# A four-layer graph network in one kernel: neighbours' lists made at fixed places of the convolution, and the attention's own rows scattered by order in the third layer's last step

## The chip, the cores and the metric

The kernel runs on one core of a Trainium2 chip. The metric is the device time of one execution in microseconds (us). The engines are TensorE (PE in the profile; PEld is its weight load), VectorE (DVE), ScalarE (ACT), GpSimd (POOL) and SyncE (SP). POOL and SP also issue DMAs: POOL the indirect ones, which gather or scatter rows of HBM by a list of row numbers, and SP the direct ones. A row L2049 of the profile is line 2049 of the kernel before.

## The reference, cut to what matters

Four layers follow one another on `x` of 8 batches x 2048 nodes x 64 features, float32, with one 0/1 adjacency `adj` (2048 x 2048). Each layer is `x = x + layer(relu(layernorm(x)))`. The change touches what surrounds layers 1 to 3:

```python
# layer 1: Chebyshev convolution, K = 3
A_stack = [I, A, 2 A A - I]
w = einsum('nd,dkio->nkio', embedding, weight); b = embedding @ bias
x_g = einsum('knm,bmc->bnkc', A_stack, x)
out = einsum('bnki,nkio->bno', x_g, w) + b
# layer 2: three steps of message passing
for _ in range(3):
    effects = einsum('nm,bmd->bnd', adj, v)
    v = relu(concat([v, effects]) @ W1.T + b1) @ W2.T + b2
# layer 3: graph attention
h = x @ weight; e_src = h @ a[:D]; e_dst = h @ a[D:]
e = adj * leaky_relu(e_src[:, :, None] + e_dst[:, None, :], 0.2)
out = softmax(e, -1) @ h + bias
```

The product of `adj` with a [2048, 64] matrix per batch is needed in layers 1 and 2 (two products in layer 1, three in layer 2), and the softmax of layer 3 runs over all 2048 nodes, those that are no neighbours having the score 0. The adjacency is sparse: only a few nodes have many neighbours.

## The kernel before

**Tiles and columns.** A node's 8 x 64 values stand in one row of 512 columns (CW). The 2048 nodes make 16 tiles of 128 (NT), and four chunks of four tiles for work that has the features on the partitions. The first tile holds the nodes with many neighbours.

**A product with the adjacency (class `Feed`).** Each of the three steps of layer 2, and each of the two products of layer 1, gathers 60 blocks of 128 rows (`raw<-sent,index`, 256 KB, L2636, on POOL), splits each into two parts (`part_hi` by ACT, L2653, `part_lo` by DVE, L2654), and multiplies both by weights of 0 and 1 on PE (`acc`, L177). There are six buffers for raws in the Chebyshev product and the steps, so a gather waits for the `part_lo` that reads the buffer's last content. Rows of nodes with many neighbours are kept in SBUF (`hub`) and are multiplied densely.

**Layer 1 (`layer1_near`, then `convolution_near`).** First the Chebyshev product over 16 tiles, then the convolution at four places, one for each chunk (order 1, 0, 2, 3). A place has four column blocks q, each with four groups (`blk`, two blocks b a group); a group makes four `pk` in PSUM by eight matmuls (six PSUM buffers, `Conv.bank`), then four `y` on DVE (L1856: (pk + bias) x emb, three buffers), each of which is added to an accumulator `half` (L1863): on POOL, but on DVE where b is the last. The second product of the adjacency runs alongside, one place ahead (`advance()`, twice a group). The layer norm of a finished chunk is done in pieces, in the following place (the list `waiting`). The first q of the first place is computed early (`Conv.first_part`, `early0_*`, `early_y`).

**Layer 2 (`layer2_near`).** Three steps over 16 tiles. The generator `neighbours` (L2015) goes along with steps 0 and 1, one piece (`near_step`) after each group of four gathered blocks. It first sorts the nodes by their number of neighbours (`ranks`, L493, a running sum by nine adds at L521; `by_rank`, L537) and stores the order in HBM (`order3`). Then, for each of tiles 1 to 15 in that order, it fetches 128 rows of 0/1 links (L2039, a POOL gather of 512 KB), multiplies them by the node's number plus one (L2043), and takes the eight greatest numbers of each row (MAX8, L2049), as often as the tile's longest list needs (one to three times), with a MATCH_REPLACE (L2052) between; a copy (L2056) puts the numbers into `near`. 15 multiplications, 21 MAX8 and 6 MATCH_REPLACE in all. In step 2, class `Scores` normalises each chunk as its rows come out, multiplies by the weight of layer 3 and writes rows of h and scores to HBM (`f_rows`, L2899 and L2900).

**Layer 3 (`layer3_near`, class `Near`).** The first tile, in the sorted order, is done densely: 16 blocks `jt`, each with 16 exponentials on ACT (L3119, L3120), a maximum and a multiplication on DVE (L3123, L3124), then a `plain` matmul and 16 recordings of `first` on PE. The other 15 tiles (`others`, in the order 15, 13, 11, 1, 10, 2, 9, 3, 8, 4, 7, 5, 6, 12, 14) go by lists: for each tile one gather of the tile's own rows (`ring<-f_rows,order`, by order) and 3 to 20 gathers of its neighbours' rows (`ring<-f_rows,near`, L2966, POOL), a softmax over the list (from `e`, L3011, to `den`), products `y` of two neighbours at a time (L3037), which PE adds up in `acc` with an identity, `o` (L3056), and a scatter of `o` to `att_rows` by order (L2977). The two generators take turns in the program. At the end `result` reads `att_rows` and adds x.

**What sets the order.** Each engine takes its instructions in order. A scheduler puts them in that order when the kernel is built, from the program's order and its own estimates of when inputs are ready; `behind` (L193) makes an instruction keep its place in the program's order on its engine. Pools of buffers (`bufs`) add waits for release.

The lines of the convolution (L1861 to L1863) and of layer 2 that hand out this work:

```python
own = b == NBLK - 1
add = nc.vector if own else nc.gpsimd
add.tensor_add(acc, acc, y)
...
for i, _ in enumerate(feed.listed(acc, t)):
    if i % feed.GROUP == feed.GROUP - 1 or i == (LISTED[t] or FAR) - 1:
        near_step()
```

Of the kernel before, what the change touches and what calls it, by code (L numbers as in the profile page):

```python
# [7 lines left out]
F = mybir.dt.float32  # L8
BF = mybir.dt.bfloat16

F12 = mybir.dt.float32r
I32 = mybir.dt.int32
# [7 lines left out]
P = 128  # L20
# [115 lines left out]
class Kernel:  # L136
# [8 lines left out]
    def __init__(self, tc, ctx, a):  # L145
# [19 lines left out]
        self.f_rows = dram.tile([N, WIDE], F, name="f_rows")  # L165
        self.att_rows = dram.tile([N, NB * D], F, name="att_rows")
# [1516 lines left out]
    def layer1_near(self, slots, k2, far):  # L1683
# [11 lines left out]
        with (  # L1695
# [4 lines left out]
            with tc.tile_pool(reuse_waits="tile", name="cheb", bufs=2) as w:  # L1700
# [13 lines left out]

                feed = Feed(self, lists, w, self.sent[0], lambda jt: ah(jt))
                for t in range(NT):
                    acc = ps.tile([P, CW], F, name="acc", bufs=2)
                    feed.target(acc, t, hub)
                    if t < HUBS:
                        nc.scalar.copy(ah(t), acc)  # L1720
                        lists.hub.fill(self, t, ah(t))
                    else:
                        feed.finish(ah(t), ah(t), acc, t)
                    nc.sync.dma_start(self.sent[1][t * P : (t + 1) * P], ah(t))
                    if t > 0:
                        turn(t - 1)
                    if t == NT // 2:
                        conv.begin()
# [5 lines left out]
    def convolution_near(self, slots, k, ps, conv):  # L1734
# [7 lines left out]
        with tc.tile_pool(reuse_waits="tile", name="conv", bufs=2) as w:  # L1742
# [62 lines left out]
            steps.prepare(bank)  # L1805
            for place, ch in enumerate(chunks):
                s = slice(ch * CW, (ch + 1) * CW)
                aah = aahs[place % 2]
                ends = place == NC - 1
                ahead = iter(()) if ends else product(place + 1)  # L1810
# [12 lines left out]
                for q in range(NP):  # L1823
# [6 lines left out]
                    for blk in range(0, NBLK, 2):  # L1830
# [17 lines left out]
                        for b in (blk, blk + 1):  # L1848
                            for half in range(2):
# [10 lines left out]
                                if new:  # L1860
                                    own = b == NBLK - 1  # L1861
                                    add = nc.vector if own else nc.gpsimd
                                    add.tensor_add(acc, acc, y)  # L1863
# [17 lines left out]
                waiting[2:2] = [first, lambda: None, lambda norm=norm: next(norm, None)]  # L1881
            while waiting:
                waiting.pop(0)()
# [19 lines left out]
    def layer2_near(self, slots, k2):  # L1903
# [3 lines left out]
        with (  # L1907
# [8 lines left out]
            near = self.neighbours(k, lambda: ps.tile([P, CW], F, name="p2"), slots)  # L1916
# [60 lines left out]
            def near_step():  # L1977
                next(near, None)

            for step in range(3):  # L1980
                if step == 2:
                    for _ in near:
                        pass
                feed = Feed(self, lists, w, self.sent[2 + step], None)
                for t in range(NT):
# [11 lines left out]
                    for i, _ in enumerate(feed.listed(acc, t)):  # L1997
                        if i % feed.GROUP == feed.GROUP - 1 or i == (LISTED[t] or FAR) - 1:
                            near_step()
                        advance(2 if step == 2 and t in (13, 14) else 1)  # L2000
# [14 lines left out]
    def neighbours(self, k, bank, slots):  # L2015

        nc = self.nc
        order = k.tile([P, 2, NT], I32, name="order")  # L2020
        w = Parts(slots.tile([P, 2 * N], F, name="sort", tag="q4"))
        rank = self.ranks(w, bank, 1, NEAR[1])
        yield
        self.by_rank(w, bank, rank, order)
        nc.sync.dma_start(self.order3, order)
        yield
        near = self.near
        words = slots.tile([P, 2, N], F, name="near_rows", tag="q4")
        rows = words[:, 0].bitcast(BF).rearrange("p (i n) -> p i n", i=2)
        named = words[:, 1].bitcast(F16).rearrange("p (i n) -> p i n", i=2)  # L2030
        words = slots.tile([P, 2, N], F, name="line", tag="q5")
        whole = words[:, 0].bitcast(I32)
        line = words[:, 1, : N // 2].bitcast(F16)
# [3 lines left out]
        for t in range(1, NT):  # L2037
            raw, row = rows[:, t % 2], named[:, t % 2]
            nc.gpsimd.indirect_dma_start(  # L2039
                raw, None, self.links[:],  # L2040
                bass.IndirectOffsetOnAxis(ap=order[:, 1, t : t + 1], axis=0),
            )
            nc.vector.tensor_mul(row, raw, line)  # L2043
# [3 lines left out]
            for i in range(most):  # L2047
                eight = top[:, 8 * i : 8 * i + 8]
                nc.vector.max(out=eight, in_=row)  # L2049
                yield  # L2050
                if i + 1 < most:
                    nc.vector.match_replace(  # L2052
                        out=row, in_to_replace=eight, in_values=row, imm_value=0.0
                    )
                    yield
            nc.vector.tensor_copy(near[:, FIRST[t] : FIRST[t + 1]], top[:, : NEAR[t]])  # L2056

# [644 lines left out]
class Conv:  # L2702
# [5 lines left out]
    def __init__(self, kern, slots, k, ps):  # L2708
# [19 lines left out]
        for j in range(2):  # L2728
# [9 lines left out]
        self.accs = [  # L2738
            [k.tile([P, CW], F, name=f"early{q}_{half}") for half in range(2)]
            for q in range(self.EARLY)  # L2740
        ]
# [21 lines left out]
    def first_part(self):  # L2763
# [3 lines left out]
        for q in range(self.EARLY):  # L2767
            for b in range(NBLK):
                for half, src in enumerate(self.xs):
# [3 lines left out]
                    y = self.k.tile([P, CW], F, name="early_y", bufs=2) if b else acc  # L2773
# [59 lines left out]
class Scores:  # L2833
# [30 lines left out]
    def chunk(self, col, first, n):  # L2864
# [18 lines left out]
        for t in range(first, first + n):  # L2883
# [17 lines left out]
            yield  # L2901

# [13 lines left out]
class Near:  # L2916
# [52 lines left out]

    def leave(self, t, o):  # L2970

        self.back.append((t, o))
# [9 lines left out]
    def block(self, t):  # L2982
# [9 lines left out]
        self.fetch(block[:, 0], self.order[:, 1, t : t + 1])  # L2992
# [5 lines left out]
    def others(self):  # L2998
# [3 lines left out]
        for place, t in enumerate(self.TILES):  # L3002
# [8 lines left out]
            nc.vector.tensor_tensor(  # L3011
                e, block[:, :, NB * D : NB * D + NB], es.unsqueeze(1).to_broadcast(full),
                op=OP.add,
# [47 lines left out]
    def first_tile(self):  # L3061
# [24 lines left out]
        self.fetch(mine, self.order[:, 1, :1])  # L3086
# [27 lines left out]
        for jt in range(NT):  # L3114
# [8 lines left out]
            nc.vector.tensor_max(m, m, m2)  # L3123
# [153 lines left out]
```

## Time and profile before

| | |
|---|---|
| three runs | 1938.78, 1944.40, 1930.53 us (median 1938.78) |
| the profiled execution, its own time | 1938.07 us |
| its span from the first to the last instruction | 1936.3 us |
| mean granted clock of TensorE | 0.933 of full speed |
| layer 0 | to about 600 us |
| Chebyshev product, its gathers | 604 to 700 us |
| convolution, places 1 to 3 | 886 to 1216 us |
| steps 0 and 1 of layer 2, their gathers | 1249.9 to 1351.6 and 1375.6 to 1475 us |
| layer 3 | 1655 to 1936 us |
| HBM traffic | 240.40 MB read, 63.14 MB written |

How to read it: busy time is the sum of an engine's instructions; a group's line gives its line in the kernel, engine, operation, what it writes <- what it reads, shapes, how often, its busy time and the mean of one in ns, then the engine's idle time just before it and whose result ended that idle time. In the table by stage each engine's column is its busy us and, in brackets, its instructions; the last three columns are the granted clock, the mean busy share of the 16 DMA engines and what they moved in GB/s.

### The profile page before, as it was taken

Reading aid. Unit: us, or ns where it says so; the run is one execution under the profiler, and the core shown is the slowest. Engines: PE = TensorE matmul, PEld = TensorE weight load, DVE = VectorE, ACT = ScalarE, POOL = GpSimd, SP = SyncE. Lnnn points to the kernel's source line nnn. Section 1 sums busy time; section 2 is a strip of 40 time slices with the busy share of each in tenths; the row PEclk is TensorE's granted clock in tenths of the full one; section 3 lists DMA queues with packets and bytes.
Section 4 is the critical chain, followed back from the end, with each engine's and each line's share of the span. In section 5 each row is a group of like instructions: output and inputs, shape, how many; then the busy total and the mean of one; then the engine's idle time right before and its main releaser. Section 6 shows DMA issues by size and latency. Waiting matters only on the chain. (4 is left out here: it accounts for less than half of the span.)

```text
span 1936.3 us, 22507 instructions
## 1 busy us (share of the span) xinstructions
PE 1695.0 (88%) x7139; PEld 972.7 (50%) x7139; DVE 1407.0 (73%) x2312; ACT 818.9 (42%) x1650; POOL 1048.6 (54%) x1007
## 2 busy tenths in 40 slices
PE   6888999998997788999999999689799899679885
PEld 2445766664334544443443444467577576345432
DVE  6888788874667688776776656788888576458874
ACT  5732544454656644222111100366666654356300
POOL 1101466677753646876656456276474641577770
PEclk8898999998987898999999989879989999789887
DMA  9741223335535864242230210478788774766665
GB/s 342 278 122 46 76 88 109 104 116 186 173 111 166 240 193 151 71 108 83 59 110 28 88 42 24 167 233 269 227 266 269 218 243 157 233 178 175 183 173 199
DMA packets 127226, 305.22 MB, mean 158 GB/s; under 512 B 29536, under 2 KB 33392, under 8 KB 121968
## 3 DMA queue, kind: packets, MB, share of 16 engines
q0 software_dynamic: 45328, 149.60, 26.2%
q1 hardware_dynamic: 79456, 149.81, 23.3%
q10 hardware_dynamic: 2304, 4.20, 0.6%
q8 instruction: 60, 0.98, 0.2%
q14 instruction: 78, 0.64, 0.1%
HBM read 240.40 MB, written 63.14 MB: 157 GB/s over the span
## 5 line engine op out<-in xcount | busy, mean ns | idle before, releaser
L2636 POOL DMA_INDIRECT raw<-sent,index x300 | 320.0, 1067 | 277.0 <-DVE part_lo L2654 114.9
L2653 ACT CAST part_hi<-raw 128x512 fp32r<-128x512 f32 x352 | 213.8, 619 | 325.6 <-PE acc L177 212.5
L2654 DVE TENSOR_TENSOR part_lo<-raw,part_hi 128x512 fp32r<-128x512 f32 x352 | 266.1, 780 | 92.3 <-ACT part_hi L2653 82.6
L177 PE MATMUL pk<-q,w 128*128 128x512 f32 (+1 forms) x768 | 303.3, 608 | 2.0 <-DVE q L1750 0.9
L1863 POOL TENSOR_TENSOR half<-half,y 128x512 f32<-128x512 f32 x180 | 230.3, 1308 | 120.2 <-DVE y L1856 119.6
L177 PE MATMUL acc<-q,ident 128*128 128x512 f32 x416 | 202.8, 613 | 23.1 <-DVE q L3056 17.0
L177 PE MATMUL acc<-part_lo,weights 128*128 128x512 f32 x365 | 167.0, 459 | 34.2 <-DVE part_lo L2654 33.7
L177 PE MATMUL acc<-part_hi,weights 128*128 128x512 f32 x365 | 173.6, 479 | 22.2 <-ACT part_hi L2653 21.7
L177 PEld LDWEIGHTS pk<-q,w 128*128 128x128 f32 (+1 forms) x768 | 115.5, 189 | 152.4 <-issue 117.4
L1856 DVE SCALAR_TENSOR_TENSOR y<-pk,bias,q 128x512 f32<-128x512 f32 x210 | 148.1, 744 | 54.9 <-PE pk L177 36.7
L2966 POOL DMA_INDIRECT ring<-f_rows,near x121 | 141.7, 1171 | 64.6 <-issue 29.2
L177 PEld LDWEIGHTS acc<-q,ident 128*128 128x128 f32 x416 | 77.0, 194 | 96.8 <-issue 42.9
L177 PEld LDWEIGHTS acc<-part_lo,weights 128*128 128x128 f32 x365 | 73.1, 200 | 87.9 <-DVE part_lo L2654 74.2
L2345 POOL TENSOR_TENSOR q<-q,beta 128x512 f32<-128x512 f32 x57 | 76.0, 1335 | 71.3 <-DVE beta L2321 32.6
L177 PEld LDWEIGHTS acc<-part_hi,weights 128*128 128x128 f32 x365 | 72.8, 199 | 71.4 <-ACT part_hi L2653 39.6
L177 PE MATMUL pp<-adj,x_ind_hi 128*128 128x512 f32 x256 | 89.5, 465 | 0.5 <-DVE q L882 0.3
L300 DVE RECIPROCAL std<-std 128x512 f32<-128x512 f32 (+1 forms) x17 | 53.8, 3162 | 32.6 <-ACT std L299 32.6
L3037 DVE TENSOR_TENSOR q<-ring,e 128x1024 f32<-128x1024 f32 x58 | 70.1, 1220 | 9.0 <-PE acc L177 8.8
L2622 ACT CAST hub_weights<-dense 128x384 fp32r<-128x384 uint8 x80 | 40.5, 511 | 84.1 <-PE acc L177 83.6
L2345 POOL TENSOR_TENSOR q<-q,coef 128x512 f32<-128x512 f32 x57 | 63.0, 1106 | 21.0 <-DVE q L2368 17.6
L2553 POOL DMA_INDIRECT listed_raw<-in_adjT_dram,cell x60 | 63.8, 1063 | 16.5 <-issue 16.1
L177 PE MATMUL pp<-adj,x_ind_lo 128*128 128x512 f32 x256 | 72.7, 403 | 0.0
(510 smaller groups left out, 3482.3 us busy)
## 6 DMA issues: line engine op xcount, KB each, us to landing
rows<-in_adj_dram SPq DMA_DIRECT2D x16, 1024.0 KB, 8.9
adj_t<-in_adjT_dram SPq DMA_DIRECT2D x64, 256.0 KB, 3.0
own<-sent SPq DMA_DIRECT2D x52, 256.0 KB, 4.1
raw<-sent SPq DMA_DIRECT2D x52, 256.0 KB, 3.5
sent<-u SPq DMA_DIRECT2D x48, 256.0 KB, 4.0
q<-x SPq DMA_DIRECT2D x9, 1024.0 KB, 5.0
links<-squares POOLq DMA_DIRECT2D x16, 512.0 KB, 8.0
sent<-q SPq DMA_DIRECT2D x32, 256.0 KB, 3.6
```

What stands on the lines that cost most here:

```text
L177: self.nc.tensor.matmul(out, lhsT, rhs, start=start, stop=stop)
L300: nc.vector.reciprocal(std, std)
L1856: nc.vector.scalar_tensor_tensor(y, pks[b, half], bias[:, b : b + 1], emb[:, b], op0=OP.add, op1=OP.mult,)
L1863: add.tensor_add(acc, acc, y)
L2345: self.nc.gpsimd.tensor_tensor(x, x, by.unsqueeze(2).to_broadcast([P, NB, D]), op=OP.mult)
L2553: self.kern.behind(nc.gpsimd.indirect_dma_start(raw[:, i], None, rows, bass.IndirectOffsetOnAxis(ap=self.cell[:, c + i : c + i + 1], axis= ...
L2622: self.nc.scalar.copy(to, self.lists.dense[:, :, i * P : (i + 1) * P])
L2636: self.nc.gpsimd.indirect_dma_start(raw, None, self.rows[:], bass.IndirectOffsetOnAxis(ap=self.lists.index[:, c : c + 1], axis=0),)
L2653: nc.scalar.copy(hi, raw)
L2654: nc.vector.tensor_sub(lo, raw, hi.bitcast(F))
L2966: self.nc.gpsimd.indirect_dma_start(to, None, self.kern.f_rows[:], bass.IndirectOffsetOnAxis(ap=index, axis=0))
L3037: nc.vector.tensor_tensor(y.rearrange("n i (b f) -> n i b f", b=NB), block[:, i : i + 2, : NB * D].rearrange("n i (b f) -> n i b f", b=NB) ...
```

## The change

1. The sort (`order_nodes`, from the first half of `neighbours`) runs in the Chebyshev product instead of at the start of layer 2, a piece after each of the tiles 2 to 4, in pools of its own. Layer 2 loads the order back, twice, by SP.
2. The lists are made in places 1 to 3 of the convolution, one piece after every group, with DVE's multiplications, MAX8 and MATCH_REPLACE kept in the program's order. A gather of links is issued one tile ahead. The rows of links share a buffer with the early part of the convolution, which is over by then.
3. The adds of the last b go to POOL, as all others.
4. In step 2, each tile's rows of h and scores are also scattered to two new tensors, `own_h` and `own_scores`, at the nodes' places in the order: 32 indirect DMAs on POOL.
5. In layer 3 the tiles' own rows are read from those by SP (two direct DMAs a tile) instead of 16 gathers on POOL; `e` and the first tile's maximum keep the program's order on DVE.

```diff
+        self.own_h = dram.tile([N, NB * D], F, name="own_h")
+        self.own_scores = dram.tile([N, 2 * NB], F, name="own_scores")
...
+                sorting = self.order_nodes(conv.bank, conv.order)
                 feed = Feed(self, lists, w, self.sent[0], lambda jt: ah(jt))
...
+                    if t > 1:
+                        next(sorting, None)
...
             for place, ch in enumerate(chunks):
...
+                if place == 1:
+                    words = k.tile([P, 4 * CW], F, name="near_rows", tag="early", bufs=1)
+                    near = self.neighbours(
+                        steps.k, conv.order, range(1, NT),
+                        words.bitcast(BF).rearrange("p (i n) -> p i n", i=2),
+                        words.bitcast(I32), w.tile([P, N], F16, name="line", bufs=1),
+                    )
...
-                                    own = b == NBLK - 1
-                                    add = nc.vector if own else nc.gpsimd
-                                    add.tensor_add(acc, acc, y)
+                                    nc.gpsimd.tensor_add(acc, acc, y)
+                        if b % 2:
+                            next(near, None)
...
-            near = self.neighbours(k, lambda: ps.tile([P, CW], F, name="p2"), slots)
+            order = k.tile([P, 2, NT], I32, name="order")
+            nc.sync.dma_start(order, self.order3)
+            self.nodes = k.tile([P, 2, NT], I32, name="order")
+            nc.sync.dma_start(self.nodes, self.order3)
...
-                    for i, _ in enumerate(feed.listed(acc, t)):
-                        if i % feed.GROUP == feed.GROUP - 1 or i == (LISTED[t] or FAR) - 1:
-                            near_step()
+                    for _ in feed.listed(acc, t):
                         advance(2 if step == 2 and t in (13, 14) else 1)
...
+    def order_nodes(self, bank, order):
+        rank = order[:, 1].bitcast(F)
+        with self.tc.tile_pool(reuse_waits="tile", name="sort", bufs=1) as w:
+            self.nc.vector.tensor_copy(rank, self.ranks(w, bank, 1, NEAR[1]))
         yield
-        self.by_rank(w, bank, rank, order)
-        nc.sync.dma_start(self.order3, order)
+        with self.tc.tile_pool(reuse_waits="tile", name="sorted", bufs=1) as w:
+            self.by_rank(w, bank, rank, order)
         yield
+        self.nc.sync.dma_start(self.order3, order)
+        yield
+    def neighbours(self, k, order, tiles, rows, whole, line):
...
+        fetch(0)
+        for i, t in enumerate(tiles):
+            fetch(i + 1)
+            row = rows[:, i % 2].bitcast(F16)
+            self.behind(nc.vector.tensor_mul(row, rows[:, i % 2], line))
             yield
...
+                self.behind(nc.vector.max(out=eight, in_=row))
                 yield
...
+        early = k.tile([P, 4, CW], F, name="early", tag="early", bufs=1)
+        self.accs, self.ys, self.turn = [[early[:, 0], early[:, 1]]], early[:, 2:], 0
+        self.order = k.tile([P, 2, NT], I32, name="order")
...
+            at = bass.IndirectOffsetOnAxis(ap=kern.nodes[:, 0, t : t + 1], axis=0)
+            nc.gpsimd.indirect_dma_start(kern.own_h[:], at, self.rows(t), None)
+            nc.gpsimd.indirect_dma_start(kern.own_scores[:], at, kern.scores[:, t], None)
...
+    def own(self, to, t):
+        dma, rows = self.nc.sync.dma_start, slice(t * P, (t + 1) * P)
+        dma(to[:, : NB * D], self.kern.own_h[rows])
+        dma(to[:, NB * D :], self.kern.own_scores[rows])
...
-        self.fetch(block[:, 0], self.order[:, 1, t : t + 1])
+        self.own(block[:, 0], t)
...
-            nc.vector.tensor_tensor(
-                e, block[:, :, NB * D : NB * D + NB], es.unsqueeze(1).to_broadcast(full),
-                op=OP.add,
+            kern.behind(
+                nc.vector.tensor_tensor(
+                    e, block[:, :, NB * D : NB * D + NB], es.unsqueeze(1).to_broadcast(full),
+                    op=OP.add,
+                )
             )
...
-        self.fetch(mine, self.order[:, 1, :1])
+        self.own(mine, 0)
...
-            nc.vector.tensor_max(m, m, m2)
+            kern.behind(nc.vector.tensor_max(m, m, m2))
```

## The prediction

> **What bounds the kernel now.** I read the page's table of engines first, then the busy time of each engine by stage, then the groups of instructions inside three stages, and last the waits of VectorE (DVE) in the fourth layer. The whole-span table says only that PE is busy 88% of the time; the stages have different limits, so the change has to be costed stage by stage.
>
> ```profile
> PE 1695.0 (88%) x7139; PEld 972.7 (50%) x7139; DVE 1407.0 (73%) x2312; ACT 818.9 (42%) x1650; POOL 1048.6 (54%) x1007
> ...
> core 0: us, PE busy (x) PEld busy (x) DVE busy (x) ACT busy (x) POOL busy (x), PEclk, DMA share, GB/s
> 604.00:700.00 96.00, 76.08 (x275) 48.74 (x273) 68.18 (x109) 64.09 (x134) 62.12 (x60) 0.90 0.82 233
> 886.00:1000.00 114.00, 113.07 (x363) 47.66 (x363) 79.60 (x102) 17.68 (x36) 73.42 (x62) 1.00 0.28 79
> 1000.00:1110.00 110.00, 108.98 (x344) 43.43 (x342) 72.86 (x95) 15.14 (x29) 60.73 (x49) 1.00 0.20 60
> 1110.00:1216.00 106.00, 103.79 (x347) 46.11 (x346) 66.37 (x94) 5.97 (x10) 57.77 (x48) 0.95 0.09 35
> 1250.00:1352.00 102.00, 87.34 (x464) 69.07 (x463) 89.91 (x122) 61.82 (x123) 72.76 (x66) 0.90 0.79 244
> 1376.00:1476.00 100.00, 86.41 (x459) 68.53 (x458) 85.33 (x115) 62.83 (x125) 73.23 (x68) 0.93 0.82 259
> ```
>
> Row 604 is the Chebyshev product, rows 886 to 1110 are places 1 to 3 of the convolution, rows 1250 and 1376 are steps 0 and 1 of the third layer. In the convolution PE is busy 326 of 330 us, and DVE only 219: DVE has 111 us to spare, POOL 138. In the two steps DVE is near 87% and POOL's DMA issues follow one another. So the change moves DVE work from two stages where DVE and POOL set the pace to one where PE does.
>
> ```profile
> L2636 POOL DMA_INDIRECT raw<-sent,index x60 | 65.1, 1085 | 33.7 <-DVE part_lo L2654 18.8 <-issue 11.0 <-DVE near L2056 1.5
> L2654 DVE TENSOR_TENSOR part_lo<-raw,part_hi 128x512 fp32r<-128x512 f32 x62 | 40.9, 690 | 12.4 <-ACT part_hi L2653 9.6 <-ACT hub_weights L2622 2.0 <-PE acc L177 0.2
> ...
> L2049 DVE MAX8 top<-q 128x8 f32<-128x2048 f16 x9 | 20.6, 2286 | 0.0
> ...
> L2043 DVE TENSOR_TENSOR q<-q,q 128x2048 f16<-128x2048 bf16 x9 | 11.0, 1217 | 0.0
> ```
>
> These are groups of step 1 (1376 to 1476). POOL's raw gathers wait 18.8 us for part_lo (the buffer it frees), and part_lo stands on DVE behind MAX8s of 2.29 us.
>
> ```profile
> L177 PE MATMUL pk<-q,w 128*128 128x512 f32 (+1 forms) x488 | 199.2, 609 | 2.0 <-DVE q L1750 0.9 <-DVE y L1856 0.7
> L1863 POOL TENSOR_TENSOR half<-half,y 128x512 f32<-128x512 f32 x136 | 173.4, 1303 | 112.5 <-DVE y L1856 112.2
> L1856 DVE SCALAR_TENSOR_TENSOR y<-pk,bias,q 128x512 f32<-128x512 f32 x158 | 111.6, 744 | 45.7 <-PE pk L177 32.2 <-POOL half L1863 11.9 <-PE side L177 0.5
> ...
> L2654 DVE TENSOR_TENSOR part_lo<-raw,part_hi 128x512 fp32r<-128x512 f32 x22 | 29.0, 1318 | 16.2 <-ACT part_hi L2653 16.2
> L1863 DVE TENSOR_TENSOR half<-half,y 128x512 f32<-128x512 f32 x24 | 26.5, 1109 | 3.0 <-POOL half L1863 1.1
> ```
>
> These are groups of the convolution's places 1 to 3. PE waited 2.0 us for anybody. The same part_lo that takes 690 ns in step 1 takes 1318 here, among POOL's adds.
>
> ```profile
> DVE e L3011 <- DMA att_rows<-o,order: 15.1, 1, 15.1
> DVE e L3011 <- DMA ring<-f_rows,near: 14.3, 3, 9.4
> ...
> DVE e L3011 <- DMA ring<-f_rows,order: 8.5, 1, 8.5
> ```
>
> These are DVE's waits in the fourth layer (waiting instruction, releaser: total us, times, longest). POOL issues 153 indirect DMAs there back to back from 1660 to 1884; the 15.1 is a tile's `e` standing at the head of DVE's queue while the first tile's work, ready, stands behind it.
>
> **The sort.** About 13.5 us of DVE (nine compares of 0.526, one of 2.29, small ones) leave the start of step 0, where they stand among 19 part_los between 1236 and 1264; the order's store on SP goes along. In the Chebyshev product DVE is busy 71%, but DMA is 0.82 and POOL issues steadily, waiting for part_lo. Hidden by DVE's 28 us of idle time it costs nothing; with the cover gone 13.5. I take +4 there. At step 0's start POOL waited up to 10.4 us on part_lo; I take -4 of it.
>
> **The convolution.** Into places 1 to 3 go on DVE 15 multiplications (1.217), 21 MAX8 (2.286), 6 MATCH_REPLACE (2.277), 15 copies (0.17), one cast (1.16): 18.3 + 48.0 + 13.7 + 2.6 + 1.2 = 83.8 us. Out go 24 adds of 1.109 (26.6). DVE: 219 + 57 = 276 of 330. Per group of four y, of which the three places have 48, that is 5.75 us where PE needs 330/48 = 6.9. POOL gets those 24 adds (1.3 each, 31 us) and 15 gathers (some 1.3 with their gap, 20 us) and an iota (1.8): 192 + 53 = 245 of 330. On the mean PE keeps its lead. It does not at the norms: the group with a MAX8 beside a reciprocal (3.3 us) and its neighbours comes to 11.4, another of the same norm to 10.7, against 7. PE has six pk banks, four of them one group's, so it can run about two banks (3.5 us) ahead of a late DVE: of the 4.4 + 3.7 us some 4 go through to PE. Three norms: 12.
>
> Here a rule speaks against the change. The row: part_lo, two inputs from SBUF, takes 1318 among POOL's adds against 690, so +0.6 us. The Trainium skill, "SBUF — State Buffer", section "Who interferes with whom", says why it may be worse: a DVE instruction with two SBUF inputs and a GpSimd instruction that reads SBUF exclude each other, and the later one is blocked for the whole of the other. The new multiplication has two SBUF inputs and 32 more adds run on POOL (30 in the places, two early ones); MAX8 and MATCH_REPLACE, with one large input, are free of it. By the row 15 x 0.6 = 9 us of DVE (285 of 330, 5.9 a group, still under 6.9); by the rule a multiplication can stand behind a run of adds, and the longest part_lo of this stage, 3.5 us, is 2.8 over its plain time, so 15 x 2.8 = 42 and DVE at 318 of 330, where PE would lose perhaps 40. I take the row, as it is this stage's mean: +12 in all, 0 to 40 for the range. A gain is excluded, since PE only idles 2 us.
>
> **Steps 0 and 1.** 14 gathers (1.07 + 0.3 gap, 19 us of POOL), the iota and about 75 us of DVE leave. The raws of step 0 take 1249.9 to 1351.6 and of step 1 1375.6 to 1475, some 102 and 100 us. POOL's own pace is 60 x (1.085 + 0.3) = 83. The nearest row is the Chebyshev product, the same 60 raws without lists: 94 us. The steps have more small matmuls (464 against 275 records), PE busy 87 at most. I take 92 each: 202 - 184 = -18. Bounds: 97 each (-8, only what POOL waited for the lists' own work), 83 each (-36). Late next is the raw's landing and the part_hi on ACT.
>
> **Step 2.** 32 scatters on POOL, about 1.35 each, 43 us. POOL is 45% busy or less from 1545 to 1600 and 5 of 40 after, PE is 95% busy, so they lie beside PE. But a scatter that waits for its rows holds the raws queued behind it, and 4 MB more are written where DMA stands at 0.78. Behind the last step's end only the pair of the last tile is left, 2.7 us. I take +3 (0 to 12). The order's two loads on SP are early and hidden.
>
> **Layer 3.** POOL loses 16 gathers (1.03 + 0.3, 22 us) of a queue that is full for 224 us. SP reads the rows instead, 32 direct DMAs, in time beside the ring's gathers. The program order on `e` and on the first tile's maximum puts three blocks of first-tile work before tile 15's `e`, which fills the 15.1 us stall; but tiles no longer overlap: each begins its softmax after the last one's `o`, a chain of 1.4 us before the first product and about as much at its end, 2.8 x 15 = 42 us in which PE has only the first tile's matmuls. Those (16 blocks of about 3.5 us with `plain`) fill most of it. Laid along DVE and PE the tiles end near 1887 instead of 1901: -14. Bounds -25 (stalls and gathers both go) and +10 (the gaps between tiles are not filled).
>
> Sum: 4 - 4 + 12 - 18 + 3 - 14 = -17 from the profiled execution's 1938.07, so 1921. That execution is 0.7 below the median of the three runs (1930.5 to 1944.4), so nothing is corrected.
>
> **Rivals.** (1) Slower: the convolution becomes bound by DVE. The place is y L1856 behind a MAX8; it decides when the groups' sum on DVE stays over 6.9 us for longer than two pk banks last. If all that was added shows, 57 + 9 = 66 in place of 12: 1975; half of that gives 1942. For it: the 11 us groups at the norms, two-input multiplications among adds. Against: 54 us of idle DVE left by the rows. (2) Little gain: the steps are held by DMA (0.8) and PE, 97 each, and layer 3's gaps eat what POOL saves (0): 1938 + 4 - 4 + 12 - 8 + 3 = 1945; with half of layer 3's gain 1938. For it: raws land late and POOL issues at its pace already; against: the Chebyshev row. (3) Large gain: steps at POOL's pace (-36), layer 3 -25, conv +5: 1938 + 5 - 36 + 3 - 25 = 1885. (4) It doesn't do what it says: if the lists fell out of the convolution into its tail, the 57 us of DVE would come after 1216. The instruction order of the changed kernel has all of them between the y's, so little is left for this.
>
> **How the numbers follow.** The summed case (1903 to 1938) has 0.48, the large gain 0.16, little gain 0.16, the slower case 0.20. A difference of 1% (19 us) is about what a measurement of this kernel can tell from no change. Faster by over 1% (under 1919): 0.16 and somewhat over half of the first, 0.28, so 0.44; slower (over 1958): of the fourth case the larger part and a little for what none of them names, 0.17; within: 0.39. The range leaves out a tenth on each side: 1890 to 1960.
>
> **What would show it.** Right: PE's idle time in the convolution's pk group grows from 2 to about 15 us, at the groups after a norm; raws of steps 0 and 1 span 90 to 95; L2043's mean in the convolution about 1.8; e L3011 waits no longer for att_rows. Wrong: PE waiting on y by 40 us or more (rival 1), raws still at 97 (rival 2), the last scatter of attention rows more than 245 us after the last step's end, as before.

## The result, and the profile after

| | before | after |
|---|---|---|
| median of the runs on one chip | 1935.08 us (4 runs) | 1969.74 us (4 runs, 1965.26 to 1972.78) |
| ratio after / before, 95% interval | | 1.0168 (1.0137 to 1.0200) |
| span of the profiled execution | 1936.3 us | 1971.0 us |
| mean granted clock | 0.933 | 0.930 |

The change makes the kernel slower by 1.7%, 33 us by the ratio. The forecast was 1921, with 1890 to 1960 as range. Set out by stages, with the start of each read from the timelines (POOL's raw gathers, SP's last write of rows of h to `f_rows`, the span's end), the two profiled executions differ so:

| stage | before | after | difference | forecast |
|---|---|---|---|---|
| first raw gather of the Chebyshev product to first raw gather of step 0 | 645.1 | 670.9 | +25.8 | +12 (sort +4 and -4, convolution +12) |
| steps 0 and 1, to the first raw gather of step 2 | 246.6 | 213.1 | -33.5 | -18 |
| step 2, to the last write of `f_rows` | 157.7 | 168.4 | +10.7 | +3 |
| layer 3, to the end | 282.1 | 314.2 | +32.1 | -14 |

(604.8 before and 604.4 after lie ahead of them.) The signs are right in three stages, and the lists' gain is even greater than forecast. Layer 3 has the wrong sign and is 46 us off.

The table by stage of the kernel after, rows in the columns shown before: two stretches of the convolution's places 1 to 3 (which run, by their first `y`, from 882, 1004 and 1122; before from 868, 982 and 1097), steps 0 and 1, step 2, the start of layer 3 and its tiles. The stretches don't hold the same work as the prediction's rows.

```profile
912.00:1033.00 121.00, 116.02 (x363) 47.98 (x362) 99.40 (x119) 18.19 (x36) 89.69 (x74) 0.99 0.29 89
1033.00:1158.00 125.00, 122.11 (x364) 49.80 (x364) 92.29 (x116) 12.63 (x24) 82.04 (x66) 0.95 0.27 78
...
1275.00:1383.00 108.00, 101.07 (x566) 81.40 (x565) 69.50 (x107) 75.68 (x151) 62.62 (x60) 0.98 0.81 255
1383.00:1488.00 105.00, 98.42 (x559) 80.97 (x559) 68.00 (x104) 75.06 (x149) 60.83 (x60) 0.97 0.81 253
...
1489.00:1657.00 168.00, 149.62 (x701) 98.04 (x701) 102.78 (x202) 87.06 (x182) 90.24 (x90) 0.96 0.68 215
1657.00:1711.00 54.00, 25.61 (x116) 16.87 (x116) 14.52 (x29) 23.33 (x68) 37.75 (x36) 0.74 0.79 254
1711.00:1937.00 226.00, 185.85 (x526) 90.68 (x526) 161.19 (x289) 74.57 (x243) 132.93 (x106) 0.89 0.50 141
```

In the first stretch of the convolution DVE now works 99.4 of 121 us (82%) and PE still 116: it is not bound by DVE. In the steps PE is at 94%, DVE at 65%. Step 2 has 90 instructions on POOL where there were 61. The row that decides is the last: from the first `e` to the last scatter 226 us pass in which nobody is busy throughout: PE 82%, DVE 71%, POOL 59%. The same stretch of the kernel before is as long, but POOL is at 74% in it:

```profile
1672.00:1901.00 229.00, 193.83 (x641) 102.65 (x641) 165.09 (x307) 96.25 (x309) 170.43 (x146) 0.91 0.61 172
```

The clocks of the two stretches, 0.89 and 0.91, make some 4 us of PE's time (an estimate: 186 x (0.91 / 0.89 - 1)).

Who waits in layer 3 of the kernel after (waiting instruction, releaser: total us, times, longest):

```profile
POOL att_rows L3000 <- DVE e L3035: 40.7, 5, 13.9
...
DVE o L3081 <- PE acc L179: 31.6, 14, 7.0
...
PE acc L179 <- DVE e L3050: 24.3, 9, 3.2
DVE q L3062 <- PE acc L179: 23.2, 19, 2.3
...
DVE q L3099 <- DMA q<-in_adj_dram,order: 18.8, 1, 18.8
...
PE acc L179 <- DVE q L3081: 12.2, 5, 3.6
```

L3035 is `e`, L3050 the last but one step of the softmax, L3081 `o` and the first two products, L3062 the products. The waits of `e` for DMAs (15.1, 14.3 and 8.5 us before) are gone, as the change meant. In their place DVE waits for PE at the end of 14 of the 15 tiles, 31.6 us (before: 3.8 in three), and PE waits for DVE at the start of the next, 24.3 + 12.2 (before, L3056 alone: 17.0). The scatters that wait for `e` are the same thing from POOL's side. DVE's timeline at one tile's end:

```profile
1726.58 2.35 DVE L3062 TENSOR_TENSOR q<-ring,e 128x1024 f32<-128x1024 f32 x2
1735.95 0.69 DVE L3081 TENSOR_TENSOR o<-acc,den 128x512 f32<-128x512 f32 x1 [7.02 <-PE acc L179]
1736.56 0.20 DVE L3035 TENSOR_TENSOR e<-ring 128x48 f32<-128x48 f32 x1
...
1738.16 0.69 DVE L3081 TENSOR_TENSOR q<-q,none 128x512 f32<-128x512 f32 x1
```

and PE's over the same time:

```profile
1726.80 3.65 PE L179 MATMUL first<-h,q 128*128 128x65 f32 x16 [0.48 <-ACT q L3145]
1730.24 5.67 PE L179 MATMUL acc<-q,ident 128*128 128x512 f32 x8
```

DVE's last products end at 1728.9. PE first does a block of the first tile, 3.65 us, that stands ahead in its queue, then eight sums, and `o` waits 7.0 us for them. Only then does the next tile's `e` begin, though no wait for its rows is recorded, and its first product starts 1.6 us later.

### The profile page after: what moved, and what is told of

The parts are those of the page before. It is cut to its first block, busy times and chain, and to the rows that moved or that the text cites. A ratio compares the mean times of both kernels' runs of the same rounds, so it can differ in the third digit from the quotient of the medians.

```text
span 1971.0 us, 22715 instructions
## 1 busy us (share of the span) xinstructions
PE 1715.7 (87%) x7139; PEld 974.4 (49%) x7139; DVE 1384.4 (70%) x2281; ACT 818.9 (42%) x1650; POOL 1099.3 (56%) x1055
## 4 chain that ended last, share of the span: by engine, by line
PE 36%; DMA 6%; DVE 5%; issue 5%; POOL 3%; ACT 2%; SPq 0%; DVEq 0%; POOLq 0%; ACTq 0%
PE pk L179 17%; PE acc L179 12%; DMA raw<-sent,index 3%; POOL raw L2650 2%; PE bank L179 1%; PE first L179 1%; PE pn L179 1%; POOL half L1874 1%; DMA q<-att_rows 1%; PE side L179 1%; PE pz L1959 1%; PE pw L179 1%; DMA q<-in_adj_dram,order 1%; DVE q L3081 1%; DVE q L3062 1%
## 5 line engine op out<-in xcount | busy, mean ns | idle before, releaser
L2650 POOL DMA_INDIRECT raw<-sent,index x300 | 311.3, 1038 | 283.7 <-DVE part_lo L2668 126.7
L179 PE MATMUL pk<-q,w 128*128 128x512 f32 (+1 forms) x768 | 311.0, 624 | 5.3 <-DVE q L1755 3.3
L1874 POOL TENSOR_TENSOR half<-half,y 128x512 f32<-128x512 f32 x210 | 263.8, 1286 | 71.3 <-DVE y L1869 70.6
L179 PE MATMUL acc<-q,ident 128*128 128x512 f32 x416 | 217.4, 655 | 40.4 <-DVE e L3050 24.3
L2983 POOL DMA_INDIRECT ring<-f_rows,near x121 | 148.1, 1224 | 49.7 <-issue 28.0
L179 PEld LDWEIGHTS acc<-q,ident 128*128 128x128 f32 x416 | 82.5, 208 | 132.9 <-issue 86.7
L3062 DVE TENSOR_TENSOR q<-ring,e 128x1024 f32<-128x1024 f32 x58 | 70.3, 1221 | 23.2 <-PE acc L179 23.2
L302 DVE RECIPROCAL std<-std 128x512 f32<-128x512 f32 (+1 forms) x17 | 53.7, 3162 | 31.6 <-ACT std L301 31.6
```

The costliest lines, as they stand in the source:

```text
L179: self.nc.tensor.matmul(out, lhsT, rhs, start=start, stop=stop)
L302: nc.vector.reciprocal(std, std)
L1874: nc.gpsimd.tensor_add(acc, acc, y)
L2650: self.nc.gpsimd.indirect_dma_start(raw, None, self.rows[:], bass.IndirectOffsetOnAxis(ap=self.lists.index[:, c : c + 1], axis=0),)
L2983: self.nc.gpsimd.indirect_dma_start(to, None, self.kern.f_rows[:], bass.IndirectOffsetOnAxis(ap=index, axis=0))
L3062: nc.vector.tensor_tensor(y.rearrange("n i (b f) -> n i b f", b=NB), block[:, i : i + 2, : NB * D].rearrange("n i (b f) -> n i b f", b=NB) ...
```

## The experiments

Two parts were taken apart: the order on DVE in layer 3 (Theory A), and the own rows that are scattered and read back (Theory B). The stages below are those of the table above, from the one profile of each run; stages that a run left as they were differ by some us between profiles (the first stage of the kernel before took 645.1 us, with only the order of layer 3 changed 643.4). The medians of the kernel before were 1939.47 us beside the first four runs and 1938.10 beside the next four.

**free_both: the change without the two orders.**

```diff
-            kern.behind(
-                nc.vector.tensor_tensor(
-                    e, block[:, :, NB * D : NB * D + NB], es.unsqueeze(1).to_broadcast(full),
-                    op=OP.add,
-                )
-            )
+            nc.vector.tensor_tensor(
+                e, block[:, :, NB * D : NB * D + NB], es.unsqueeze(1).to_broadcast(full),
+                op=OP.add,
+            )
...
-            kern.behind(nc.vector.tensor_max(m, m, m2))
+            nc.vector.tensor_max(m, m, m2)
```

> The changed kernel, with the two orders of DVE in layer 3 (on e and on the first tile's maximum) left to the scheduler. Theory A (the strict order costs: a tile's softmax can't begin before the last tile's o, and tile 15 waits for three first-tile blocks): layer 3, 314 us from the last write of f_rows to the end, falls back to 282 or less, the time to some 1937, and DVE's e begins its first tile near 1672 to 1680 instead of 1711. Theory B (the scattered own rows and SP's late reads hold the tiles): the time stays within 8 us of 1970, and e waits for own_h or own_scores.

1927.65 us, 0.9943 of the kernel before (0.9925 to 0.9961); layer 3 is 279.8 us, `e` begins at 1672.3. Theory A holds. Without those orders the rest of the change is a gain.

**before_order: the kernel before with the two orders alone** (the same diff the other way round, in the kernel before).

> The kernel before with nothing but the two orders on DVE in layer 3. Theory A: the strict order is costly by itself, so the time rises by 20 to 35 us, to 1955 to 1970, all of it in layer 3. Theory B (the order only costs together with own rows by SP): within 8 us of 1936.

1966.72 us, 1.0143 (1.0113 to 1.0172): 27 us, and layer 3 is 314.3, as in the whole change. The order needs no scattered rows to cost that. Its waits are the same ones:

```profile
DVE o L3058 <- PE acc L177: 33.4, 14, 7.4
...
PE acc L177 <- DVE e L3027: 24.2, 9, 3.1
```

**free_max: only the order on the first tile's maximum taken away.**

```diff
-            kern.behind(nc.vector.tensor_max(m, m, m2))
+            nc.vector.tensor_max(m, m, m2)
```

> The changed kernel with the order on the first tile's maximum alone left to the scheduler; e keeps the program's order. If what costs is the order on e (tiles that don't overlap), the time stays within 6 us of 1970. If what costs is that the first tile's blocks 0 to 2 stand before tile 15's e, some 20 to 30 us come back: 1940 to 1950.

1966.92 us, 1.0146 (1.0118 to 1.0174), layer 3 323.6: nothing comes back. With `e` held in the program's order, each tile still stands in full behind the one before, and the first tile's blocks still stand ahead of tile 15 (three maxima of blocks before its `e`, at 1703.0). The order on `e` is enough to cost it all: against free_both, which ran on the same chip and differs in this order alone, 39 us. Whether the order on the maximum alone costs anything was not run.

**pipelined: the order on `e` kept, but in a program in which tiles overlap** (lists as in the change, own rows gathered as before). The softmax becomes a method, and the next tile's is written ahead of the last products of the current one.

```diff
+        soft = self.softmax(self.TILES[0], ready.pop(0))
         for place, t in enumerate(self.TILES):
+            block, e, none, den = soft
...
+                if i == range(-1, n, 2)[-2] and ready:
+                    soft = self.softmax(self.TILES[place + 1], ready.pop(0))
                 for j in range(min(2, n - i)):
                     kern.mm(acc, kern.ident, y[:, j], start=i + j < 0, stop=i + j == n - 1)
```

> lists_only with the order on e kept, but the program itself puts the next tile's softmax ahead of the current tile's last products, so that tiles overlap. Theory A (what costs in the strict order is that no tile's softmax starts before the last tile's o): the tiles' part, 226 us under the strict order, falls by 15 tiles x 2 to 2.5 us, to about 190, though it starts 25 to 35 us late behind the first tile's blocks; layer 3 about 280, the time 1915 to 1930. If the order costs by its late start alone, layer 3 stays near 310 and the time near 1955.

1921.75 us, 0.9930 (0.9890 to 0.9970): as fast as lists_only below (0.9926), which is the same kernel without the order and with the softmax where it was. From the first `e` to the last scatter 200 us pass (1684.1 to 1884.2), against 231 in before_order and 226 in the change, though not the 190 expected. Layer 3 takes 279.6 us, although `e` begins 43 us after the last write of `f_rows` (before: 18). So the late start alone is not what costs, and the same order, held by the same means, costs nothing on balance when the next softmax stands before the current `o`. What the new place of the softmax would give without the order was not run; a small cost of the order may hide behind such a gain. The waits at the tiles' ends shrink:

```profile
DVE q L3065 <- PE acc L179: 15.1, 18, 2.9
...
PE acc L179 <- DVE q L3065: 11.8, 9, 4.1
...
PE acc L179 <- DVE q L3086: 6.4, 8, 1.2
...
DVE o L3086 <- PE acc L179: 5.5, 4, 2.7
```

(L3065 the products, L3086 `o` and the first two.) The timeline shows the interleaving; the softmax (L3028 to L3045) is done before `o`:

```profile
1842.13 0.24 DVE L3028 TENSOR_TENSOR e<-ring 128x80 f32<-128x80 f32 x1 [4.21 <-DMA ring<-f_rows,order]
...
1842.83 1.22 DVE L3065 TENSOR_TENSOR q<-ring,e 128x1024 f32<-128x1024 f32 x1
...
1846.49 0.16 DVE L3045 SCALAR_TENSOR_TENSOR den<-none,den 128x8 f32<-128x8 f32 x1
1847.71 0.69 DVE L3086 TENSOR_TENSOR o<-acc,den 128x512 f32<-128x512 f32 x1 [1.06 <-PE acc L179]
```

**lists_only: sort, lists and adds as in the change; no scatter, no own rows by SP, no order on DVE in layer 3.**

```diff
-            at = bass.IndirectOffsetOnAxis(ap=kern.nodes[:, 0, t : t + 1], axis=0)
-            nc.gpsimd.indirect_dma_start(kern.own_h[:], at, self.rows(t), None)
-            nc.gpsimd.indirect_dma_start(kern.own_scores[:], at, kern.scores[:, t], None)
...
-        self.own(block[:, 0], t)
+        self.fetch(block[:, 0], self.order[:, 1, t : t + 1])
```

> Only the lists' part of the change: sort in the Chebyshev product, lists in the convolution, all adds on POOL; own rows gathered on POOL in layer 3, no scatter in step 2, no order on DVE in layer 3. Theory A's ledger by stages (sort and convolution +25 up to the first gather of step 0, steps 0 and 1 -33, step 2 and layer 3 as before): 1936 + 25 - 33 = 1928, and step 2's 60 gathers last 106 us as before instead of 123. Rival C (the lists' gain in the steps is given back in step 2, which PE bounds, whoever scatters): 1936 or more.

1923.32 us, 0.9926 (0.9903 to 0.9949). By stages: 660.7, 212.2, 155.4, 278.8, so +16, -34, -2, -3 (the profiled execution, 1914.85, was the fastest of the six). The lists' part alone gains 14 us by the ratio; rival C falls. Step 2's gathers take 104 us.

**rows_only_free: only the own rows, in the kernel before** (scatters in step 2 and reads by SP as in the change's diff; no order on DVE).

> The kernel before with only the own rows' part: 32 scatters in step 2, own rows read by SP in layer 3, no order on DVE, lists still made in steps 0 and 1. From the ledger of the first four runs (with scatters, step 2 lasts 167 and 168 us from its first gather to the last write of f_rows against 155 and 158 without; layer 3 280 against 279): this part costs 8 to 12 us and saves none, so 1944 to 1951. If the rows by SP do save POOL's 16 gathers (22 us) where the lists don't stand: 1925 or less.

1945.49 us, 1.0033 (1.0018 to 1.0047): 6 us lost. The stages are 647.9, 243.7, 171.1, 274.5: step 2 pays 13.4 us, layer 3 gets 7.6 back. So by these two profiles taking 16 gathers from POOL does help layer 3, by a third of their 22 us, and the scatters cost more than that.

**scatter_late: free_both, with the scatters of tiles 0 to 11 behind the last raw gather** (`True` keeps them at their place in the program's order on POOL).

```diff
-            nc.gpsimd.indirect_dma_start(kern.own_h[:], at, self.rows(t), None)
-            nc.gpsimd.indirect_dma_start(kern.own_scores[:], at, kern.scores[:, t], None)
+            if t >= 12:
+                self.scatter(t)
...
                     late.append((step, t, z))
+            for t in range(12):
+                last.scatter(t, True)
             turn(*late[-1])
```

> free_both (the changed kernel without the two orders) with the scatters of tiles 0 to 11 issued after the last raw gather of step 2, in POOL's program order. Theory H (the scatters cost because raws stand behind a scatter that waits for its rows): step 2's 60 gathers last 106 us again instead of 123 and the time falls by 8 to 12 us, to 1917. Theory D (4 MB more written slow the gathers down, or POOL's time itself): within 4 us of free_both's 1928, or above it, since 31 us of issues then stand just ahead of the ring's gathers.

1925.23 us, 0.9927 (0.9908 to 0.9945). H is right about where the time went and wrong about the total: the 60 gathers take 104 us (free_both: 123.6) and step 2 155.4 (167.0), but layer 3 grows from 279.8 to 285.4, since the ring's first gather comes 16 us after the last write of `f_rows` where it came 9 after. The time did not fall by the 8 to 12 us expected: the ratios, with overlapping intervals, don't tell the two apart. In free_both POOL's timeline shows the scatters among the raws:

```profile
1550.21 0.98 POOL L2917 DMA_INDIRECT own_h<-q,order  x1 [0.38 <-DMA own_h<-q,order]
1551.93 0.97 POOL L2918 DMA_INDIRECT own_scores<-scores,order  x1 [0.73 <-DMA own_scores<-scores,order]
1553.20 0.98 POOL L2650 DMA_INDIRECT raw<-sent,index  x1 [0.30 <-issue]
...
1561.38 0.98 POOL L2917 DMA_INDIRECT own_h<-q,order  x1 [1.16 <-DMA own_h<-q,order]
```

A scatter takes POOL as long as a gather (0.98 and a gap), and often waits also for the scatter before it into the same tensor to land. In the change this shows at the end of step 2 as well, where one `own_scores` waited 3.40 us for another.

**lists_dve: lists_only with the last b's adds back on DVE.**

```diff
-                                    nc.gpsimd.tensor_add(acc, acc, y)
+                                    own = b == NBLK - 1
+                                    add = nc.vector if own else nc.gpsimd
+                                    add.tensor_add(acc, acc, y)
```

> lists_only with the last b's adds back on DVE (32 adds). If moving them was needed for the lists to fit (DVE 276 + 27 of 330 us in places 1 to 3), the convolution gets 5 to 15 us longer: 1928 to 1938. If DVE had room enough, within 4 us of 1923, and POOL's relief gains nothing.

1919.81 us, 0.9898 (0.9854 to 0.9942), with the first stage 660.4 against 660.7: DVE had room for lists and adds together. No gain from the move of the adds shows.

The last four runs fell on chips on which the kernel before itself takes 1989 and 1984 us; only ratios, and kernels run together, are compared.

**sort_only: only the sort in the Chebyshev product, the lists in the steps as before.**

```diff
+                sorting = self.order_nodes(conv.bank, conv.order)
...
+                    if t > 1:
+                        next(sorting, None)
```

> Only the sort's move: order_nodes in the Chebyshev product as in the change, but the lists made in steps 0 and 1 as before, adds, scatter, own rows and layer 3 as before. The other runs with the sort there take 97 to 102 us for the product's 60 gathers against 89 to 93, and 82 to 86 instead of 80 from there to the first y of the places. If the sort is the cause of both, the first gather of step 0 comes 5 to 10 us later than before's at most, the steps take 240 to 246, the time is 1938 to 1948. If something else in the lists' part does it (the shared tile of the early adds), the product itself stays at 93 and the time within 4 us of 1938.

0.9987 (0.9967 to 1.0006): no cost that can be measured. The product's 60 gathers took 102 us here, but the chip was slower. Besides the sort this kernel has the shared buffer of the convolution's early part, and issues the gathers of links one tile ahead, so it can't tell the sort from that buffer; what makes the product 4 to 9 us longer in the other runs stays open.

**pipelined_early: pipelined, adds on DVE, and tile 15's softmax ahead of the first tile's blocks.**

```diff
         ready = [self.block(t) for t in self.TILES[:2]]
+        soft = self.softmax(self.TILES[0], ready.pop(0))
         yield
-        soft = self.softmax(self.TILES[0], ready.pop(0))
```

> pipelined with the adds of the last b on DVE, and with the first list tile's softmax ahead of the first tile's blocks in the program. pipelined's tiles begin 43 us after the last write of f_rows, lists_only's 16. If the late start is what is left of the order's cost, layer 3 gets 10 to 20 us shorter than 280: the time 1900 to 1912. If POOL's queue of ring gathers (220 us, then the last tiles) holds layer 3 now, it stays at 275 to 280: 1916 to 1922.

0.9950 (0.9930 to 0.9970). lists_dve did not run on that chip; on another, both ran together:

> lists_dve once more, beside pipelined_early on one chip, since the last call's chip took 1989 us for the kernel before. 0.988 to 0.993 of the kernel before, as the first time.

> Against lists_dve on the same chip. If the late start was left of the order's cost: 8 to 15 us under lists_dve. If POOL's queue of ring gathers holds layer 3: within 4 us of it.

lists_dve_2 took 1971.97 us, 0.9946 (0.9926 to 0.9965), above the 0.988 to 0.993 expected; pipelined_early_2 1969.97, 0.9946 (0.9923 to 0.9968): 2 us apart. In pipelined_early_2 POOL's ring gathers run from 1675.1 to 1910.2 and the end comes 53 us later. On these chips the early start brings nothing that can be measured. That POOL's queue is the reason isn't shown: no run took load off it, and right after the early softmax DVE stands idle for a reason that the profile doesn't give (in lists_dve_2 for 21.5 us, in pipelined_early_2 longer):

```profile
1727.78 0.69 DVE L3088 TENSOR_TENSOR q<-q,none 128x512 f32<-128x512 f32 x1 [31.96 <-issue]
```

No profile from the faster chips has such a wait, and there pipelined_early was not run.

## Why the prediction was wrong, point by point

**Layer 3, -14 forecast, +32 measured: the step that failed.** The prediction saw that "tiles no longer overlap", priced it at 2.8 x 15 = 42 us, and then let the first tile's matmuls "fill most of it", so that the tiles "end near 1887". They ended at 1937. The gaps were priced somewhat high, but that they would be filled was wrong, and so was the place of the stall that the order was to fill.
- The gaps stayed. The tiles' part took 226 us in the change and 231 in before_order; let overlap, it takes 200 (pipelined), so the gaps are worth 26 to 31 us, about 2 a tile where 2.8 was forecast. The first tile's blocks did not fill them. While there were blocks left (1711 to 1868), DVE still waited 17.2 us for PE at the ends of eight tiles, and PE 20.9 us for DVE at the starts. A block can also stand ahead of the sums that `o` waits for (1726.80). For the last five tiles none was left: the last four scatters, from 1900 on, stand 15, 11 and 10 us apart. In free_max the maxima of the blocks were free to move on DVE; the blocks were then used up by 1812, and layer 3 was no shorter.
- The late start. Three blocks ahead of tile 15's `e` were to fill the 15.1 us stall. But tile 15 is the first of the lists' tiles, and in the kernel before its `e` began with no idle time right ahead of it; the stall stood before the fourth tile's, 45 us later:

```profile
1672.17 0.19 DVE L3011 TENSOR_TENSOR e<-ring 128x32 f32<-128x32 f32 x1
...
1717.05 0.33 DVE L3011 TENSOR_TENSOR e<-ring 128x168 f32<-128x168 f32 x1 [15.12 <-DMA att_rows<-o,order]
```

In the kernel after, tile 15 waits behind those blocks, and they wait for their exponentials:

```profile
1698.35 1.23 DVE L3148 TENSOR_TENSOR q<-q 128x1024 f32<-128x1024 f32 x1 [8.31 <-ACT q L3145]
...
1703.02 1.23 DVE L3148 TENSOR_TENSOR q<-q 128x1024 f32<-128x1024 f32 x1 [2.19 <-ACT q L3145]
...
1708.26 1.22 DVE L3148 TENSOR_TENSOR q<-q 128x1024 f32<-128x1024 f32 x1 [0.43 <-ACT q L3145]
...
1710.66 0.18 DVE L3035 TENSOR_TENSOR e<-ring 128x32 f32<-128x32 f32 x1
```

So `e` began 53 us after the last write of `f_rows`, where it was 18 before and 46 in before_order. Some 8 us of that come from the first tile's own row of links: DVE begins with it (L3099) 23 us after that write, 15 in the two others.
- Why both count. In the kernel before the tiles' part is no shorter, 229 us, but there it waits for POOL's gathers (`e` alone 38 us for DMAs): the last gather is issued 55 us before the end, and so in lists_only (55) and pipelined (53). In the change it is issued 83 us before the end, in before_order 76: now the chain of tiles through DVE and PE ends last. What the stalls gave up, the gaps took. A strict order with an early start was not run, so the 32 us can't be split between the two terms.

The -14 also contained the 16 gathers taken from POOL. Without the order on DVE they are worth 7.6 us by one profile (rows_only_free), and with lists in the convolution nothing shows (279.8 in free_both, 278.8 in lists_only).

The parts don't add up to the whole: the order alone costs 27 us in the kernel before, the rows 6, the lists give 14 back, which makes +19 where the change has +33. Part of the difference is the order itself: free_max, with the order on `e` alone, is 39 us slower than free_both on the same chip. By the profiles both orders cost layer 3 about the same in both places (32 us from before to before_order, 34 from free_both to the change); why the times differ more is open.

**Convolution, +12: near in number, the mechanism only in small part.** The first stage costs 12 to 26 us in the seven profiles of kernels with the lists there that were taken before the slower chips, where +12 was summed. The forecast's reason was that PE waits for late `y`s. PE's idle time in the pk group did not grow to 15 us, but to 5.3:

```profile
L179 PE MATMUL pk<-q,w 128*128 128x512 f32 (+1 forms) x475 | 196.4, 616 | 5.3 <-DVE q L1755 3.3 <-DVE y L1869 1.7
...
L2056 DVE TENSOR_TENSOR near_rows<-near_rows,line 128x2048 f16<-128x2048 bf16 x14 | 17.0, 1217 | 0.0
L2668 DVE TENSOR_TENSOR part_lo<-raw,part_hi 128x512 fp32r<-128x512 f32 x20 | 14.7, 735 | 3.0 <-ACT part_hi L2667 2.9
```

These are groups of 912 to 1240, most of places 1 to 3 after. By the first `y` of each place, the four places got 3, 8, 3 and -1 us longer, 13 in all. Of the 10 in places 1 to 3, PE's idle time makes half (9.2 us after, 4.2 before) and longer matmuls the other half (PE busy 348.8 us, 343.8 before); why these are longer is open. That the four places come near 12 is therefore luck in the main. A further 11 us lie ahead of them: the Chebyshev product's gathers take 99.2 instead of 93.4 us, and from there to the first y of the places 85.8 pass instead of 80.1. The sort was forecast to cost 4 and to give 4 back at the start of step 0; nothing came back there (36 us from the last y to the first gather, 35 before).

**The rule weighed against the row.** The prediction took 0.6 us a multiplication from the row of part_lo and held 2.8 open by the rule of two SBUF inputs. The row did not come true at all, the rule once: 14 of the 15 multiplications take 1210 to 1224 ns, what they took in the steps. The first one, at the start of place 1, lies among four adds of POOL that end at 895.93, and ends 1.1 us after them:

```profile
890.99 4.94 POOL L1874 TENSOR_TENSOR half<-half,y 128x512 f32<-128x512 f32 x4
...
892.97 4.05 DVE L2056 TENSOR_TENSOR near_rows<-near_rows,line 128x2048 f16<-128x2048 bf16 x1
```

It took 2.8 us more than its plain time, and it took some 4.05 us in all ten profiles of kernels with the lists there. Beside the 14 others no add ran, or only the last part of one. part_lo fell from 1318 to 735 ns in the mean. So the rule's price for one clash was right and the number of clashes was not 15: instructions that may exclude each other cost only where they meet, and in this stage that is 2.8 us and not 42.

**Steps 0 and 1, -18 forecast, -33.5 measured.** The choice was the Chebyshev product's 94 us as nearest row, against POOL's pace of 83 as bound. The gathers took 83.5 and 82.3 us from first to last: the bound. The lists' gathers left POOL, the raw gathers became shorter (1044 and 1014 ns, before 1121 and 1085), and POOL's waits for part_lo inside a step, as far as they exceed the 0.3 us that passes before nearly every gather, fell from 8.2 and 5.4 us to 3.8 and 4.5. (Of the 18.8 us that the prediction read for step 1, 10.4 stand ahead of the step's first gather.)

**Step 2, +3 forecast, +10.7 measured.** The head-of-line wait was named and priced too low. Scatters among the raws cost 10 to 13 us there, and moved behind them 6 at the start of layer 3.

**The rivals.** The slower case was expected in the convolution, from y behind a MAX8. The kernel became slower, but not there. The place was foreseen only in the little-gain rival ("layer 3's gaps eat what POOL saves"), priced at 0 in all. The sign that the prediction gave for being wrong there came true: the last scatter of attention rows was issued 279 us after the last write of `f_rows`, over the 245 named (before: 246).

## What to carry to other kernels

An order forced on one engine made each unit of work here as long as its whole chain over all engines; it cost nothing on balance once the program itself wrote the next unit's first steps ahead of the current one's last. When gaps are "filled by other work", check in the instruction order of every engine that this work can still move into them, and that there is enough of it to the end; and when a stall is to be filled, that the new work stands before the instruction that stalls. A combined change should be costed and run by parts: here one part gained 0.7%, one lost 0.3%, and two lines of ordering lost 1.4%.

## What the runs showed of the hardware that was not expected

Chips differ: the kernel before took 1935 to 1939 us in three sets of runs and 1984 and 1989 in two others. In the profile from the slower chip of lists_dve_2, the 60 gathers of steps 0 and 1 took 91 and 98 us where lists_dve's took 85 and 82. All four profiles from the slower chips have an idle time of DVE of 21 to 33 us in the first 60 us of layer 3 whose end the profile puts down to nothing that it knows; in the ten others layer 3 has none over 6 us. What it is stays open. Absolute times from different sets were therefore not compared.
